# Modulated 1-D convolutions on one core: the whole of G ahead of the eviction of S, VectorE's side work at the iteration's end

## Chip, cores and metric

The kernel runs on one core of a Trainium2 chip. The metric is the device time of one execution in microseconds (us). All times below are us unless marked ns. The engines are TensorE (PE; its weight loads are listed as PEld), VectorE (DVE), ScalarE (ACT), GpSimd (POOL) and SyncE (SP, which issues the DMAs).

## What is computed

For 128 samples of 64 channels by 1024 positions, four convolution layers (64 to 64 channels, three taps, the weights scaled per sample by a style vector and then normalised per output channel) are chained, and the input is added to the result. The types are same, upsample (stride 2 transposed, then blurred), same, downsample (blurred, then stride 2). No nonlinearity stands between them.

```python
s = style @ mw.T + mb
weight = SCALE * w * s[:, None, :, None]
demod = lax.rsqrt(jnp.sum(weight * weight, axis=(2, 3)) + EPS)
weight = weight * demod[:, :, None, None]
...
for i, typ in enumerate(TYPES):
    out = _layer(out, style, weights[i], biases[i], mod_w[i], mod_b[i], typ)
...
x = x + _L0_cond_ref(x, cond_512, ...)
```

## The kernel before

**The idea.** Since nothing nonlinear stands between the layers, the kernel multiplies the four layers' weights together for each sample, into one filter of nine taps, and applies that to the input. Only the few positions at both row ends, where the padding of the single layers shows, are computed apart, layer by layer, for all samples at once ("row ends").

**The work of one sample group.** Samples are taken four at a time: q counts 32 groups (NQ). A group has two rows r or s of results, each in its own PSUM bank. The steps, with the names in the code:

- `scale3`, `stage1_a`, `stage1_b` (lines 415, 461, 473): the weights of the last two layers are multiplied on TensorE into psS (line 428). ScalarE evicts four blocks of S (line 399), VectorE evicts two more in two instructions, one per bank (line 481: "the eviction of S"), GpSimd then adds two blocks of S (line 484). The bank pair of psS is the pool `ps_w`, which has one buffer: psS, psR and psW of the different groups take turns in it.
- `share_sums`, `share`, `share_copy` (lines 499, 515, 524): in some iterations part of stage 2 is computed once for several blocks: VectorE adds blocks of S (line 501), TensorE multiplies them into spare columns of psA (line 506), and ScalarE copies the result into a new psR (line 529), which lies in the banks that psS has just left.
- `stage2_rest` or `stage2_taps` (lines 535, 577): TensorE multiplies S with the blurred second layer E onto psR (line 506, or 589 without sharing); ScalarE evicts R (line 399).
- `r_sums` (GpSimd, line 638), `stage3_b`, `stage3_a` (TensorE, line 621): the first layer's weights come in; ScalarE evicts the filter Wf.
- `combine_a`, `combine_b` (VectorE): sums of filter taps, H.
- `in_g01`, `in_g2`, `in3`, `in04`, `in1`, `in2`: the input X of a group lies as three planes of every third position. VectorE makes the planes of G from X, one in `in_g2` (684 elements in each partition) and two in `in_g01` (1376), both line 712; then T3 = X − X (`in3`, line 761), T04 (`in04`, line 790), and on GpSimd T12 (`in1`, line 776, and `in2`, line 781), which need G. G has one buffer, X two.
- `conv0` to `conv4` (line 803): TensorE multiplies the five T with Wf or H into psA and Y, in the manner of a fast convolution with five products for three outputs. `sum1` (line 851) and `sum2` (lines 860 and 862) combine these on VectorE; `outputs` (line 880) scales them on ScalarE and starts the stores.

**The order.** Nothing is scheduled automatically: each engine does its instructions in the order in which the code issues them, and semaphores make it wait for others. `turn_of(q)` (line 1483) is one iteration: it works for group q (last products), n = q + 1 (first products), c = q + 2 (stages 2 and 3, input) and s = q + 4 (stage 1). It runs for q = 4 to 28; q = 4 is the entry (`entry`), and 0 to 3 and the last three groups have code of their own. Sharing is on for 4 < q < 28 (line 1370).

**Side work.** The row ends and the per-sample constants of later groups are spread over the iterations. `SIDE` (line 1334) is a table from q to a few VectorE instructions: for q = 4 the last step of an inverse root (`var_newton`), for 5 to 7 `small_rest` (for 7 also `table_b` on GpSimd), for 8 to 27 pieces of the row ends (13 `setup1`, none for 14 and 19). In iterations 4, 5 and 6 there is also a memset of some columns of Y (line 1524), onto which the small matmuls (`small`, line 1290) add later in the iteration. In 10, 14, 15 and 19 TensorE does row-end matmuls (`SLOTS`, line 1271) behind the sharing matmuls.

**Where it stands.** On VectorE one iteration is: `sum2`, `combine_a` and `combine_b`, `in04`, `share_sums`, `in_g2`, then `side(SIDE, q)` and the memset, then the eviction of S, then `in_g01`, `sum1`, `in3`, and the next iteration's `sum2`. On TensorE it is stage 2 of c, conv2 of q, stage 3, conv4, conv3 of n, stage 1, conv0, the rest of stage 1, the sharing matmuls, conv1 of n, the small matmuls, and again stage 2.

Of the kernel before, what the change touches and what calls it, by code (L numbers as in the profile page):

```python
# [63 lines left out]
def kernel(  # L64
# [18 lines left out]
    nc_v, nc_a, nc_g = nc.vector, nc.scalar, nc.gpsimd  # L83
# [57 lines left out]
    def load(q, planes=slice(0, 3), cs=range(2)):  # L141

        if q < NQ:
            at = slice(planes.start * PL, planes.stop * PL)
            for c in cs:
                nc.sync.dma_start(Xs[q % NX][:, c, at], x[2 * q + c, :, at])
# [165 lines left out]
    def var_newton(bs, ls=slice(0, NL)):  # L312

        newton(var[:, ls, bs], dm[:, ls, bs], nw[:, ls, bs])
# [44 lines left out]
    def table_b(bs):  # L359
        table(nc_g, tb, bs, slice(0, 2), slice(2, 4), oc[:, bs], 1.0)  # L360
# [199 lines left out]
    def stage2(q, pool=None, engs=(nc_a, nc_a), between=None):  # L560
        if q in shared_ps:
            ps = stage2_rest(q)
        else:
            ps = opened.pop(q, None)
            taps = range(9) if ps is None else range(3, 9)
            ps = stage2_taps(q, taps, ps or unit(pool or ps_w, f"psR{q}"))
        if between:
            between()
        t = r_pool.tile([P, 2, 9, C], F32, tag="R", name=f"R{q}")
        for r in range(2):  # L570
            scaled_copy(engs[r], flat(t[:, r, :7]), ps[r][:, : 7 * C], tC[:, q, r : r + 1])
        chain[q] = t
        return ps
# [62 lines left out]
    def r_sums(q, eng):  # L636
        t = chain[q]
        eng.tensor_add(t[:, :, 7:9], t[:, :, 2:6:3], t[:, :, 3:7:3])
# [3 lines left out]
    def stage3_b(q, ps):  # L642

        new_w(q)
        t = chain[q]
        plan = (
            (slice(0, 3), w0s[2][:, 2, :], slice(0, 7, 3)),
            (slice(0, 2), w0s[2][:, 1, :], slice(1, 5, 3)),
            (slice(0, 2), w0s[2][:, 0, :], slice(2, 6, 3)),
            (slice(3, 4), w0s[0][:, 0, :], slice(0, 1)),  # L650
            (slice(4, 5), w0s[1][:, 0, :], slice(1, 2)),
            (slice(4, 5), w0s[1][:, 1, :], slice(0, 1)),
            (slice(5, 7), w0s[0][:, 1, :], slice(7, 9)),
        )
        for i, (at, weight, slots) in enumerate(plan):
            same_row(blocks(ps, at), weight, t, slots, i == 0, i == len(plan) - 1)
        pw = shared_w[q] = unit(ps_w, f"psW{q}")
        src = blocks(ps, slice(5, 7))
        for i, f in enumerate((1.0, 1.0 / 3.0)):
            for dst, v in zip(blocks(pw, slice(i, i + 3, 2)), src):  # L660
                scaled_copy(nc_a, dst, v, f)
        stage3_out(q, ps, 0, 5)
# [48 lines left out]
    def sum_of(out, x, f, y, op=ALU.add):  # L711
        nc_v.scalar_tensor_tensor(out, x, f, y, op0=ALU.mult, op1=op)  # L712
# [6 lines left out]
    def combine_a(q):  # L719

        chain.pop(q)
        a, b, c, h1, h2, h3 = taps(q)
        sum_of(h1, c, -2.0, a)
        residual(q)
        sum_of(h3, h1, 1.0 / 6.0, b)

    def combine_b(q, steps=range(3)):

        a, b, c, h1, h2, h3 = taps(q)
        plan = (h2, c, -0.5, a), (h1, b, -3.0, h2, ALU.subtract), (h2, h2, -1.0 / 3.0, b)  # L730
        for i in steps:
            sum_of(*plan[i])
# [10 lines left out]
    def plane(buf, i, pairs=BOTH_PAIRS):  # L743

        at = PL * (2 - i) if i < 3 else PL * 2 + 1
        return buf[:, pairs, at : at + NJ]

    def t_tile(q, tag):
        if (q, tag) not in Ts:
            Ts[q, tag] = tpool.tile([P, 2, 1 + (tag != "T3"), PL], F32, tag=tag, name=f"{tag}_{q}")  # L750
        return Ts[q, tag]

    def g_tile(q):
        if q not in Gs:
            Gs[q] = gpool.tile([P, 2, 3 * PL], F32, tag="G", name=f"G{q}")
        return Xs[q % NX], Gs[q]
# [6 lines left out]
    def in_g01(q, pairs=BOTH_PAIRS):  # L763
        if q < NQ:
            X, g = g_tile(q)
            sum_of(g[:, pairs, PL:], X[:, pairs, : 2 * PL], 0.5, X[:, pairs, PL:], ALU.subtract)
# [6 lines left out]
    def in1(q, eng):  # L773
        if q < NQ:
            t, g = t_tile(q, "T12"), Gs[q]
            eng.tensor_add(t[:, :, 0, :NJ], plane(g, 2), plane(g, 1))  # L776

    def in2(q, eng):
        if q < NQ:
            t, g = t_tile(q, "T12"), Gs[q]  # L780
            eng.tensor_sub(t[:, :, 1, :NJ], plane(g, 2), plane(g, 1))  # L781
# [46 lines left out]
    def open_a(q):  # L828
        A[q] = ps_conv.tile([P, 2, 512], F32, tag="u", name=f"psA{q}")
        return banks(q)  # L830
# [22 lines left out]
    def conv2(q, *groups):  # L853
        product(q, 2, banks(q), groups or range(K))

    def sum2(q, steps=(0, 1)):
        if 0 in steps:
            m3 = m3c.pop(q)
            for s, a in enumerate(banks(q)):
                sum_of(Y[:, s, :NB], m3[:, s], 3.0, a[:, :NB])  # L860
        for s, a in parts(q) if 1 in steps else ():
            nc_v.tensor_sub(y1w[q][:, s], y1w[q][:, s], a)

    def conv4(q, *groups):
        product(q, 4, Y_banks, groups or range(K))

    def conv0(q, *groups):
        product(q, 0, banks(q), groups)
# [149 lines left out]
    def setup_x(h):  # L1018
        bs = slice(h * HB, (h + 1) * HB)
        nc_v.tensor_tensor(Xm[:, bs], Xe[:, bs], spread(sc[:, 0, bs], 8), op=ALU.mult)  # L1020
# [43 lines left out]
    def add0(s):  # L1064
        dst = Ye[s][:, :, 1:7]
        nc_v.tensor_tensor(dst, dst, spread(c0, 6), op=ALU.add)
# [211 lines left out]
    def high(n):  # L1278
        return Y[:, 1, NB + 4 : NB + 4 + n]

    SMALL = {
        1: (0, PART[1]),
        2: (1, PART[1]),
        3: (2, PART[1]),
        4: (0, REST),
        5: (1, REST),
        6: (2, REST),
    }
# [10 lines left out]
    def small_rest(q):  # L1299
        l, bs = SMALL[q]  # L1300
        const_rest(l, bs, high(bs.stop - bs.start))

    def layers(i, j):
        return REST, slice(i, j)
# [19 lines left out]
    def last_factors():  # L1324
# [9 lines left out]
    SIDE = {  # L1334
        4: lambda: var_newton(*layers(3, 4)),
        5: lambda: small_rest(4),
        6: lambda: small_rest(5),
        7: lambda: (small_rest(6), table_b(REST)),
        8: lambda: setup_x(0),
        9: lambda: setup_x(1),  # L1340
        10: setup0,
        11: lambda: add0(0),
# [21 lines left out]
    def side(work, q):  # L1364
        work.get(q, lambda: None)()
# [117 lines left out]
    def turn_of(q):  # L1483
        n, c, s = q + 1, q + 2, q + 4
        entry = q == FIRST
        stage2(c)
        if entry:
            sum2(q)
            conv4(q)
            combine_a(n)  # L1490
            r_sums(c, nc_v)
        else:
            conv2(q)
            r_sums(c, nc_g)
            sum2(q)
            in2(n, nc_g)
        side(TABLES, q)
        for i in range(3):
            load(c + 1, slice(i, i + 1))
        stage3_b(c, open_a(n))  # L1500
        if entry:
            conv0(q, 0, 1)
        else:
            combine_a(n)
            conv4(q)
        stage3_a(c)
        combine_b(n)
        conv3(n)
        if entry:
            copy_m3(n)  # L1510
            stage1_a(s)
        outputs(q, 2)
        if not entry:
            if s < NQ:
                stage1_a(s)
            copy_m3(n)
        in04(n)
        if sharing(q):
            share_sums(c + 1)
        in_g2(c)  # L1520
        side(SIDE, q)
        if q in SMALL:
            l, bs = SMALL[q]
            nc_v.memset(high(bs.stop - bs.start), 0.0)
        conv0(q, *((2,) if entry else range(K)))
        if entry:
            conv1(n, 0, 1)
        outputs(q, 1)
        if s < NQ:
            stage1_b(s)  # L1530
        in_g01(c)
        if sharing(q):
            share(c + 1, banks(q))
            share_copy(c + 1)
        outputs(q, 0)
        if q in SLOTS:
            matmuls, width, rest = SLOTS[q]
            slot(matmuls, width, Y_banks)
            rest()
        if s == NQ:  # L1540
            slot(ends3, 3, unit(ps_w, "psE"), 3)
            rest3()
        conv1(n, *((2,) if entry else range(K)))
        if q in SMALL:
            small(q)
        sum1(n)
        in3(c)
        side(LATE, q)
        if s == NQ:
            in04(c)  # L1550
        in1(c, nc_g)
        if s + 1 < NQ:
            scale3(s + 1)

# [5 lines left out]
    q, n, c = NQ - 3, NQ - 2, NQ - 1  # L1560
# [32 lines left out]
    q, n = NQ - 2, NQ - 1  # L1593
# [128 lines left out]
```

## Time and profile before

| | before |
|---|---|
| device time, median of 3 runs | 475.72 us (475.56 to 475.97) |
| span of the profiled execution | 475.5 us |
| PE busy | 469.7 us, 99% of the span |
| weight loads (PEld) | 349.5 us, 74% |
| VectorE busy | 417.3 us, 88% |
| ScalarE busy | 312.0 us, 66% |
| GpSimd busy | 165.8 us, 35% |

The span runs from the first to the last instruction of one profiled execution; the device time of that execution is not listed apart from the three runs, whose lowest is 475.56. A row of a time line reads: start, length, engine, line, operation, what it writes `<-` what it reads, shapes, number of instructions merged into the row, and in brackets the idle time of the engine just before, with the engine, tile and line that ended it. Rows of weight loads show when TensorE takes up a step better than those of matmuls, whose ends are modelled. An ordinary iteration in the middle of the span lasts 13.84 us.

### The profile page before, as it was taken

Reading aid. Unit: us, or ns where it says so; the run is one execution under the profiler, and the core shown is the slowest. Engines: PE = TensorE matmul, PEld = TensorE weight load, DVE = VectorE, ACT = ScalarE, POOL = GpSimd, SP = SyncE. Lnnn points to the kernel's source line nnn. Section 1 sums busy time; section 2 is a strip of 40 time slices with the busy share of each in tenths; the row PEclk is TensorE's granted clock in tenths of the full one; section 3 lists DMA queues with packets and bytes.
Section 4 is the critical chain, followed back from the end, with each engine's and each line's share of the span. In section 5 each row is a group of like instructions: output and inputs, shape, how many; then the busy total and the mean of one; then the engine's idle time right before and its main releaser. Section 6 shows DMA issues by size and latency. Waiting matters only on the chain.

```text
span 475.5 us, 26771 instructions
## 1 busy us (share of the span) xinstructions
PE 469.7 (99%) x11932; PEld 349.5 (74%) x11932; DVE 417.3 (88%) x694; ACT 312.0 (66%) x711; POOL 165.8 (35%) x200
## 2 busy tenths in 40 slices
PE   9999999999999999999999999999999999999996
PEld 6987788777678876677776677766788787876653
DVE  3889998879989998899979899979998999999896
ACT  4565657577766676766667666667666777766464
POOL 3634033664444342233432233422333423243200
PEclk9999999999999999999999999999999999999999
DMA  5237456535445554345544454543555544455225
GB/s 176 71 115 224 150 151 180 152 113 177 139 145 166 166 166 136 123 150 169 163 150 126 130 168 152 178 124 121 152 164 169 164 145 147 148 152 161 80 91 193
DMA packets 52707, 70.71 MB, mean 149 GB/s; under 512 B 6000, under 2 KB 50672, under 8 KB 52592
## 3 DMA queue, kind: packets, MB, share of 16 engines
q1 hardware_dynamic: 52368, 68.78, 46.3%
q8 instruction: 93, 1.52, 1.4%
q10 hardware_dynamic: 224, 0.22, 0.1%
q14 instruction: 22, 0.18, 0.1%
HBM read 35.36 MB, written 33.62 MB: 145 GB/s over the span
## 4 chain that ended last, share of the span: by engine, by line
PE 99%; DVE 0%; ACT 0%; issue 0%
PE psA L803 47%; PE Y L803 12%; PE psR L506 9%; PE psW L621 7%; PE psA L621 7%; PE psS L428 6%; PE psR L589 5%; PE psA L506 2%; PE Y L1044 2%; PE Y L183 1%; PE Y L379 1%; PE psM L220 0%; PE psE L1044 0%; PE Y L255 0%; DVE o L882 0%; PE psM L255 0%
## 5 line engine op out<-in xcount | busy, mean ns | idle before, releaser
L803 PE MATMUL psA<-T,H 64*64 64x340 f32 x2304 | 185.9, 446 | 0.0
L803 PEld LDWEIGHTS psA<-T,H 64*64 64x64 f32 x2304 | 90.7, 133 | 46.9 <-issue 2.5
L712 DVE SCALAR_TENSOR_TENSOR G<-X 128x1376 f32<-128x1376 f32 (+2 forms) x65 | 78.0, 1206 | 0.2
L776 POOL TENSOR_TENSOR T<-G 128x684 f32<-128x684 f32 x28 | 46.3, 1652 | 73.7 <-DVE G L712 73.7
L484 POOL TENSOR_TENSOR S<-S 128x128 f32<-128x128 f32 x28 | 21.6, 772 | 139.7 <-ACT S L399 139.6
L399 ACT ACTIVATE R<-psR,tC 128x448 f32<-128x448 f32 x63 | 36.6, 631 | 43.6 <-PE psR L506 25.8
L803 PE MATMUL psA<-T,Wf 64*64 64x340 f32 x768 | 63.7, 446 | 0.0
L803 PE MATMUL Y<-T,Wf 64*64 64x340 f32 x768 | 62.4, 451 | 0.0
L712 DVE SCALAR_TENSOR_TENSOR Y<-m,psA 128x340 f32<-128x340 f32 x62 | 32.0, 516 | 28.2 <-PE psA L803 26.9
L399 ACT ACTIVATE psW<-psA 128x128 f32<-128x128 f32 x100 | 19.3, 268 | 49.1 <-PE psA L621 45.0
L790 DVE TENSOR_TENSOR T<-G 128x1368 f32<-128x1368 f32 (+1 forms) x33 | 50.8, 1541 | 0.0
L399 ACT ACTIVATE Wf<-psW,t 128x256 f32<-128x256 f32 (+2 forms) x76 | 32.7, 480 | 26.7 <-PE psW L621 26.4
L761 DVE TENSOR_TENSOR T<-X 128x684 f32<-128x684 f32 x32 | 47.7, 1492 | 0.0
L506 PE MATMUL psR<-S,E 64*64 64x64 f32 (+1 forms) x1472 | 46.8, 237 | 0.0
L781 POOL TENSOR_TENSOR T<-G 128x684 f32<-128x684 f32 x28 | 46.5, 1660 | 0.0
L428 PEld LDWEIGHTS psS<-wd,w2n 64*64 64x64 f32 x1120 | 35.1, 133 | 12.9 <-issue 0.3
L506 PEld LDWEIGHTS psR<-S,E 64*64 64x64 f32 x1472 | 39.5, 134 | 4.9 <-ACT psR L529 0.2
L803 PEld LDWEIGHTS Y<-T,Wf 64*64 64x64 f32 x768 | 30.3, 132 | 16.8
L803 PEld LDWEIGHTS psA<-T,Wf 64*64 64x64 f32 x768 | 29.8, 133 | 14.5
L880 ACT ACTIVATE o<-psA,tb,td 128x340 f32<-128x340 f32 x63 | 37.1, 648 | 5.0 <-PE psA L803 2.8
L880 ACT ACTIVATE o<-y,tb,td 128x340 f32<-128x340 f32 x62 | 38.5, 678 | 0.0
L880 ACT ACTIVATE o<-Y,tb,td 128x340 f32<-128x340 f32 x62 | 36.1, 639 | 2.8 <-PE Y L803 2.0
(180 smaller groups left out, 840.4 us busy)
## 6 DMA issues: line engine op xcount, KB each, us to landing
out<-o SPq DMA_DIRECT2D x191, 170.0 KB, 2.6
X<-in_x SPq DMA_DIRECT2D x150, 172.0 KB, 3.4
X<-in_x SPq DMA_DIRECT2D x14, 516.0 KB, 5.0
par<-in_params SPq DMA_DIRECT2D x3, 192.0 KB, 3.8
Xe<-in_x_ends SPq DMA_DIRECT2D x1, 512.0 KB, 4.5
out<-Oe SPq DMA_DIRECT2D x2, 96.0 KB, 2.1
out<-o ACTq DMA_DIRECT2D x1, 170.0 KB, 2.8
par<-in_params SPq DMA_DIRECT2D x1, 160.0 KB, 2.7
```

What stands on the lines that cost most here:

```text
L399: nc_a.activation(dst, src, AF.Copy, scale=f)
L428: nc.tensor.matmul(ps[r][cols, at * C : (at + n) * C], weight[rows], wd[c if r == 0 else 1 - c][rows, taps], start=first, stop=last, skip_ ...
L506: nc.tensor.matmul(dst[r][cols], weight[rows], st[c if r == 0 else 1 - c][rows, slots, :], start=False, stop=last, skip_group_check=True,)
L589: nc.tensor.matmul(ps[r][cols, lo * C : (lo + m) * C], E[rows, e + 2, :], src[rows, a, :], start=(n == 0), stop=(n == 8), skip_group_check ...
L621: nc.tensor.matmul(dst[r][cols], weight[rows], t[rows, c, slots, :], start=first, stop=last, skip_group_check=True,)
L712: nc_v.scalar_tensor_tensor(out, x, f, y, op0=ALU.mult, op1=op)
L761: nc_v.tensor_sub(t[:, pairs, 0, :NJ], plane(X, 3, pairs), plane(X, 1, pairs))
L776: eng.tensor_add(t[:, :, 0, :NJ], plane(g, 2), plane(g, 1))
L781: eng.tensor_sub(t[:, :, 1, :NJ], plane(g, 2), plane(g, 1))
L790: nc_v.tensor_sub(t[:, pairs, :, :NJ], both(a, PL), both(b, 1))
L803: nc.tensor.matmul(ps[s][cols, :NB], w, Ts[q, tag][rows, c, i, g : g + NB], start=(g == 0 and (m == 3 or alone)), stop=(g == K - 1), skip_ ...
L880: nc_a.activation(dst, src, AF.Identity, bias=add, scale=d3)
```

## The change

`in_g01(c)` moves from behind `stage1_b` to just behind `in_g2(c)`, so VectorE makes all of G in one piece and evicts S after it. The side work of iteration q moves to the end of iteration q − 1, behind T3 and, in the program, behind GpSimd's `in1`; only the entry does its own in the old place (now behind `in_g01`), and its successor's at its end. The memset of Y moves behind the eviction of S. No instruction is added or removed, and the orders of TensorE, ScalarE and SyncE are the same; on GpSimd only the two instructions of `table_b` move, from behind `in2` and three small factors of iteration 7 to behind `in1` of iteration 6.

```diff
@@ turn_of(q) @@
         in_g2(c)
-        side(SIDE, q)
-        if q in SMALL:
-            l, bs = SMALL[q]
-            nc_v.memset(high(bs.stop - bs.start), 0.0)
+        in_g01(c)
+        if entry:
+            side(SIDE, q)
         conv0(q, *((2,) if entry else range(K)))
         if entry:
             conv1(n, 0, 1)
         outputs(q, 1)
         if s < NQ:
             stage1_b(s)
-        in_g01(c)
+        if q in SMALL:
+            l, bs = SMALL[q]
+            nc_v.memset(high(bs.stop - bs.start), 0.0)
         if sharing(q):
...
         if s == NQ:
             in04(c)
         in1(c, nc_g)
+        side(SIDE, q + 1)
         if s + 1 < NQ:
             scale3(s + 1)
```

VectorE in the middle of iteration 18, before. L501 is `share_sums`, the two G are `in_g2` (342 in two halves) and `in_g01` (688 in two halves), L1102 is the side work, L481 the eviction of S, y is `sum1`, T is T3, Y is `sum2`:

```order
L501 TENSOR_TENSOR S_5374<-S_5374 128x2x128
L712 SCALAR_TENSOR_TENSOR G_5652<-X_105 128x2x342
L1102 SCALAR_TENSOR_TENSOR Ue_162<-b1s,Ue_162 64x64 x2
L1102 SCALAR_TENSOR_TENSOR Ue_163<-b1s,Ue_163 64x64 x2
L481 SCALAR_TENSOR_TENSOR S_5644<-psS_0_5630,tB,S_5644 128x128
L481 SCALAR_TENSOR_TENSOR S_5644<-psS_1_5631,tB,S_5644 128x128
L712 SCALAR_TENSOR_TENSOR G_5652<-X_105 128x2x688
L712 SCALAR_TENSOR_TENSOR y_19_5718<-psA_5537,m_19_5647 128x680
L761 TENSOR_TENSOR T_20_5720<-X_105 128x2x342
```

The same place of the changed kernel (the numbers in the names differ a little):

```order
L501 TENSOR_TENSOR S_5375<-S_5375 128x2x128
L712 SCALAR_TENSOR_TENSOR G_5656<-X_105 128x2x342
L712 SCALAR_TENSOR_TENSOR G_5656<-X_105 128x2x688
L481 SCALAR_TENSOR_TENSOR S_5648<-psS_0_5634,tB,S_5648 128x128
L481 SCALAR_TENSOR_TENSOR S_5648<-psS_1_5635,tB,S_5648 128x128
L712 SCALAR_TENSOR_TENSOR y_19_5718<-psA_5541,m_19_5651 128x680
L761 TENSOR_TENSOR T_20_5720<-X_105 128x2x342
```

The two instructions of the eviction now stand behind 1376 elements of G in each partition where four short ones stood; those four are done at the end of iteration 17, behind that iteration's T3. VectorE in iteration 4 (the entry), as a difference of the two orders; L279 to L281 are `var_newton`, L1524 and L1532 the memset of Y:

```order
 L712 SCALAR_TENSOR_TENSOR G_1828<-X_105 128x2x342
+L712 SCALAR_TENSOR_TENSOR G_1828<-X_105 128x2x688
 L279 TENSOR_TENSOR nw<-dm,var 128x96
 L280 SCALAR_TENSOR_TENSOR nw<-nw,dm 128x96
 L281 SCALAR_TENSOR_TENSOR dm<-nw,dm 128x96
-L1524 MEMSET Y 128x96
 L481 SCALAR_TENSOR_TENSOR S_1818<-psS_0_1804,tB,S_1818 128x128
 L481 SCALAR_TENSOR_TENSOR S_1818<-psS_1_1805,tB,S_1818 128x128
-L712 SCALAR_TENSOR_TENSOR G_1828<-X_105 128x2x688
+L1532 MEMSET Y 128x96
```

The memset has gone from ahead of the eviction to behind it, and G's second instruction the other way.

## Prediction

> **What bounds the kernel now.** I read the page's chain first, then busy time by stretches of one iteration, then the time lines of VectorE, ScalarE and TensorE's weight loads inside it. The chain that ended last is TensorE almost alone:
>
> ```profile
> PE 99%; DVE 0%; ACT 0%; issue 0%
> ```
>
> The next view cuts two neighbouring iterations at VectorE's first subtraction into Y (`sum2`), the one spot where it waits for TensorE each time. Columns: stretch, its length, then busy time of PE, PEld, DVE, ACT, POOL.
>
> ```profile
> 277.73:291.57 13.84, 13.84 (x392) 9.79 (x388) 13.01 (x19) 9.86 (x23) 4.80 (x5) 1.00 0.51 161
> 291.57:305.52 13.95, 13.95 (x392) 10.13 (x388) 13.35 (x22) 9.86 (x23) 4.87 (x5) 1.00 0.49 150
> ```
>
> The first is iteration 17, the second iteration 18. PE is busy throughout both, yet the second is 0.11 longer with the same 392 matmuls. So "busy" hides a stall, and the stall is what this change works on. VectorE in iteration 17, from the G plane of `in_g2` on:
>
> ```profile
> 284.44 0.86 DVE L712 SCALAR_TENSOR_TENSOR G<-X 128x684 f32<-128x684 f32 x1
> 285.22 1.01 DVE L1093 SCALAR_TENSOR_TENSOR Ue<-b1s,Ue 128x576 f32<-128x576 f32 x1
> 286.25 0.61 DVE L481 SCALAR_TENSOR_TENSOR S<-psS,tB,S 128x128 f32<-128x128 f32 x2
> 286.78 1.58 DVE L712 SCALAR_TENSOR_TENSOR G<-X 128x1376 f32<-128x1376 f32 x1
> 288.28 0.86 DVE L712 SCALAR_TENSOR_TENSOR y<-psA,m 128x680 f32<-128x680 f32 x1
> 289.05 1.85 DVE L761 TENSOR_TENSOR T<-X 128x684 f32<-128x684 f32 x1
> 291.57 0.52 DVE L712 SCALAR_TENSOR_TENSOR Y<-m,psA 128x340 f32<-128x340 f32 x1 [0.67 <-PE psA L803]
> ```
>
> VectorE runs without a gap until 290.90 and then waits 0.67 for TensorE. What hangs on the eviction of S: ScalarE's `share_copy` (L529) writes psR into the PSUM banks that psS held, and TensorE's stage 2 (L506) adds onto what it wrote. The same iteration:
>
> ```profile
> 286.69 0.63 ACT L529 COPY psR<-psA 128x256 f32<-128x256 f32 x2 [0.24 <-DVE S L481]
> ...
> 287.39 0.44 PEld L506 LDWEIGHTS psR<-S,E 64*64 64x64 f32 x8
> ...
> 288.53 1.65 POOL L776 TENSOR_TENSOR T<-G 128x684 f32<-128x684 f32 x1 [2.92 <-DVE G L712]
> ```
>
> TensorE takes up stage 2 at 287.39, just after the copy. Iteration 18, with longer side work, shows what follows when S is later:
>
> ```profile
> 300.48 0.61 DVE L481 SCALAR_TENSOR_TENSOR S<-psS,tB,S 128x128 f32<-128x128 f32 x2
> ...
> 300.92 0.63 ACT L529 COPY psR<-psA 128x256 f32<-128x256 f32 x2 [0.62 <-DVE S L481]
> ...
> 301.33 0.41 PEld L506 LDWEIGHTS psR<-S,E 64*64 64x64 f32 x6 [0.23 <-ACT psR L529]
> ...
> 305.52 0.52 DVE L712 SCALAR_TENSOR_TENSOR Y<-m,psA 128x340 f32<-128x340 f32 x1 [0.39 <-PE psA L803]
> ```
>
> Here S starts 8.91 after the Y subtraction (300.48 − 291.57), the first stage 2 weight load comes 0.85 later (301.33) and waits for the copy, and the next Y subtraction comes 5.04 after S (305.52 − 300.48). In iteration 17 S came at 8.52 (286.25 − 277.73) and cost nothing: there the load stands at 9.66 (287.39 − 277.73), TensorE's own pace. **So S has until about 9.66 − 0.85 = 8.81; each later microsecond is a microsecond on the iteration.**
>
> **The change, part by part.** *G ahead of S.* `in_g2` ends at 285.30. Before, 0.95 of side work stood between it and S; now 1.58 of `in_g01` does. S then starts at 286.88 at the earliest, 9.15 after the Y subtraction. But GpSimd's addition in S (L484) falls into just this place. Iteration 10, where the side work holds the same instruction twice, shows what it does to the VectorE instruction behind `in_g2`:
>
> ```profile
> 182.25 0.86 DVE L712 SCALAR_TENSOR_TENSOR G<-X 128x684 f32<-128x684 f32 x1
> ...
> 182.59 0.83 POOL L484 TENSOR_TENSOR S<-S 128x128 f32<-128x128 f32 x1 [5.15 <-ACT S L399]
> ...
> 183.03 0.47 DVE L1025 TENSOR_TENSOR a<-dm 64x64 f32<-64x64 f32 x1
> 183.43 0.18 DVE L1026 COPY c<-c0f 64x64 f32<-64x64 f32 x1
> 183.62 0.22 DVE L1025 TENSOR_TENSOR a<-dm 64x64 f32<-64x64 f32 x1
> ...
> 187.13 0.44 PEld L506 LDWEIGHTS psR<-S,E 64*64 64x64 f32 x8
> ```
>
> The first copy of L1025, beside GpSimd's addition, took 0.47, the second, after it, 0.22: a hold of 0.25. Will `in_g01` be held too? Ends: 0 and 0.25, taken 0.25, since it too reads two tensors of SBUF and takes the very place of the held row.
> The Trainium skill ("SBUF — State Buffer", section "Who interferes with whom") says that a VectorE instruction with two SBUF inputs and a GpSimd instruction that reads SBUF exclude each other, the one that starts first holding the port to its end. By that rule the hold is there; an estimate without the rule would be the 9.15 above. This trace agrees with it in the 0.47 against 0.22.
> So S starts at 9.15 + 0.25 = 9.40, and with iteration 18's 5.04 behind it an iteration lasts 14.44 instead of 13.84: **+0.60** (+0.35 without the hold). The delay doesn't pile up: the next iteration's VectorE work starts from its own Y subtraction, which waits for TensorE.
>
> How many iterations? `share_copy` runs in 23 of them, two copies each:
>
> ```profile
> L529 ACT COPY psR<-psA x46: 347/360/387, 114.5 to 428.4; 128x256 f32<-128x256 f32 x46
> ```
>
> Four of these (10, 14, 15, 19) have the row-end matmuls between the sharing matmuls and stage 2. In iteration 10 `in_g2` ends at 183.11; S would start at 183.11 + 1.83 = 184.94 and the load could follow at 185.8, well before 187.13: nothing lost. Of the 19 left, iteration 18 already pays 0.11, so it adds 0.49; 5 and 6 have a memset and small matmuls (below); 16 are plain: 16 × 0.60 = 9.6.
>
> *The memset of Y behind S* (iterations 4, 5, 6). The small matmuls (L1295) wait for it, and TensorE reaches stage 2 only behind them. Iteration 4, with no sharing:
>
> ```profile
> 100.74 0.14 DVE L1524 MEMSET Y<- 128x96 f32 x1 [2.39 <-ACT o L880]
> 100.79 0.53 DVE L481 SCALAR_TENSOR_TENSOR S<-psS,tB,S 128x128 f32<-128x128 f32 x2
> ...
> 100.99 0.22 PEld L1295 LDWEIGHTS Y<-c0f,wsum 64*64 64x64 f32 x4 [0.46 <-issue]
> 101.13 0.17 PEld L589 LDWEIGHTS psR<-S,E 64*64 64x64 f32 x2
> ```
>
> The memset's start moves from 100.74 to behind S, at the latest 101.32: between nothing, if S no longer waits and starts earlier, and 0.58. Stage 2 waits for all of S anyway, so I take 0.35. In 5 and 6 S ends at about 10.0 after the Y subtraction, the memset at 10.1, the small load can come at 10.2 (0.11 behind it, as in iteration 4), and stage 2 a further 0.14 to 0.30 behind (101.13 − 100.99 here, 129.81 − 129.51 in iteration 6):
>
> ```profile
> 129.51 0.42 PEld L1295 LDWEIGHTS Y<-cc,wsum 64*64 64x64 f32 x4
> 129.81 0.29 PEld L506 LDWEIGHTS psR<-S,E 64*64 64x64 f32 x8
> ```
>
> With the Y subtraction of iteration 6 at 119.86 its stage 2 load stood at 9.95; it would stand at 10.35 to 10.5: 0.5 each, 1.0 for both.
>
> *Side work behind T3*: costed at nothing. VectorE now ends S at 10.0, waits for the conv1 result, and does `sum1` (0.86). T3 took 1.85 because GpSimd's T12 sum (288.53 to 290.18) ran beside it; that sum now starts about 1.2 earlier, right behind G, so T3 should need about 0.87, like the G plane of equally many elements. VectorE is then through with T3 near 12.1 and with 1.4 of side work at 13.5, before the Y subtraction at 14.44. Were that cover gone, the side work's whole length would delay sum2, 0.7 to 1.4 an iteration. GpSimd's part of it, `table_b` of iteration 7, is moved ahead of `r_sums`:
>
> ```profile
> L332 POOL TENSOR_SCALAR tb<-oc 64x48 f32<-64x48 f32 x2 | 0.7, 342 | 5.4 <-DVE oc L977 5.3
> ```
>
> Two short ones of 0.34, behind a T12 sum that ends earlier. The loads of X only find their planes read sooner.
>
> Sum: 9.6 + 0.5 + 1.0 + 0.35 = 11.45. The profiled span of 475.5 lies 0.2 under the median of 475.72. So 475.7 + 11.4 = **487.1**.
>
> **Rivals.**
> 1. *No hold on `in_g01`*: +0.35 an iteration: 16 × 0.35 + 0.24 (iteration 18) + 0.6 + 0.35 = 6.8, **482.5**. For it: no G instruction stands behind L484 in this trace. Against: the 0.25 above.
> 2. *The S eviction itself is held* by the T12 sum, which now starts 0.17 behind G (288.53 against 288.36). S's second half would wait out 1.65 of it, about 1.5 more in each of 19 iterations, about 28 on top: **515**. Against: `sum1` at 288.28, also PSUM with SBUF, took 0.86 beside the same sum, no longer than its elements need.
> 3. *TensorE doesn't stall*, or the edit leaves S's start where it was because S waits for something later anyway: **475.8**. Against: iteration 18 lost 0.11 at a delay of only 0.39 more.
> 4. *Faster*: T3 loses its wait for GpSimd, 1.85 − 0.87 = 0.98 in each iteration. If VectorE paced the iteration, that would outweigh the 0.60, and the 16 plain ones would gain 0.38 each: **469.6**. It decides as soon as the Y subtraction no longer waits for TensorE. In the rows it waits 0.67 and 0.39, so VectorE's time is spare there.
> The same rule of the Trainium skill (section "Who interferes with whom") stands behind rival 4: it frees T3 once GpSimd is done earlier, and the trace agrees that T3 is long only beside the sum.
>
> **How the numbers follow.** The forecast has a chance of 0.75, rival 1 0.11, rival 2 0.03, rival 3 0.05, rival 4 0.06. About 0.2% (0.95) is what a measurement can tell from no change. Faster is rival 4, 0.06; same is rival 3, 0.05; slower is the rest, 0.89. The forecast itself reaches from 484.5 (memsets free, some iterations late on TensorE's own account) to 490 (0.7 an iteration); with rival 1 the range is 481 to 490, which leaves out rivals 2, 3 and 4 and the edges.
>
> **What would show it.** Plain iterations of 14.4 instead of 13.84; S about 9.4 after the Y subtraction, G's big instruction at 1.83 instead of 1.58; each L529 waiting for S, and PEld L506 with a wait for L529 in about 19 iterations; T3 near 0.87; the wait of the Y subtraction for PE longer than 0.9. Iterations 10, 14, 15 and 19 unchanged. I am wrong if stage 2's load stays at 9.66, or if the Y subtraction stops waiting for TensorE.

## The result, and the profile after

The changed kernel takes **483.97 us** (median of 4 runs, 483.51 to 485.05), the kernel before 475.85 us beside it (4 runs, 475.56 to 477.07): a ratio of 1.0162, 95% interval 1.014 to 1.0183, or 8.1 us slower. The profiled execution took 484.11 us with a span of 482.3 us.

The same two iterations as in the prediction, 17 and 18, cut at the Y subtraction (stretch, length, then busy time of PE, PEld, DVE, ACT, POOL; the last three columns are the granted TensorE clock, the DMA engines' busy share and GB/s):

```profile
281.07:295.35 14.28, 14.28 (x392) 10.63 (x388) 12.35 (x23) 9.86 (x23) 4.79 (x5) 1.00 0.51 152
295.35:309.75 14.40, 14.32 (x392) 10.62 (x388) 11.52 (x19) 9.86 (x23) 4.92 (x5) 1.00 0.49 158
```

They were 13.84 and 13.95. PE still reads as busy all through, with the same 392 matmuls and the granted clock at 1.00: the loss doesn't show in PE's share (99% before and after), only in the lengths. VectorE in iteration 17:

```profile
287.43 0.42 DVE L501 TENSOR_TENSOR S<-S 128x256 f32<-128x256 f32 x1
287.76 2.63 DVE L712 SCALAR_TENSOR_TENSOR G<-X 128x684 f32<-128x684 f32 x2
290.32 0.59 DVE L481 SCALAR_TENSOR_TENSOR S<-psS,tB,S 128x128 f32<-128x128 f32 x2
291.34 0.87 DVE L712 SCALAR_TENSOR_TENSOR y<-psA,m 128x680 f32<-128x680 f32 x1 [0.43 <-PE psA L803]
292.12 0.86 DVE L761 TENSOR_TENSOR T<-X 128x684 f32<-128x684 f32 x1
292.90 1.12 DVE L1102 SCALAR_TENSOR_TENSOR Ue<-b1s,Ue 64x64 f32<-64x64 f32 x4
295.35 1.07 DVE L712 SCALAR_TENSOR_TENSOR Y<-m,psA 128x340 f32<-128x340 f32 x2 [1.32 <-PE psA L803]
```

The eviction of S starts 9.25 after the Y subtraction (290.32 − 281.07), where it was 8.52. The copy and the weight load behind it, and GpSimd:

```profile
290.74 0.63 ACT L529 COPY psR<-psA 128x256 f32<-128x256 f32 x2 [0.94 <-DVE S L481]
```
```profile
291.15 0.41 PEld L506 LDWEIGHTS psR<-S,E 64*64 64x64 f32 x6 [0.55 <-ACT psR L529]
```
```profile
288.13 0.81 POOL L484 TENSOR_TENSOR S<-S 128x128 f32<-128x128 f32 x1 [5.21 <-ACT S L399]
290.56 1.64 POOL L776 TENSOR_TENSOR T<-G 128x684 f32<-128x684 f32 x1 [1.62 <-DVE G L712]
```

The load comes 0.83 behind S, at 10.08 instead of 9.66, and now waits for the copy; the next Y subtraction comes 5.03 behind S (295.35 − 290.32). The table of waits says the same over the whole span (total, times, longest):

```profile
DVE Y L712 <- PE psA L803: 45.2, 28, 2.5
...
ACT psR L529 <- DVE S L481: 21.9, 23, 1.1
...
PEld psR L506 <- ACT psR L529: 9.1, 17, 0.7
```

Seventeen waits of stage 2 for the copy: the 16 plain iterations and iteration 18. VectorE's own wait for PE has grown by 18.3 to 45.2 us (26.9 before): it has more time to spare than before, not less. The page's chain speaks of less:

```profile
PE 36%; DVE 1%; issue 0%; ACT 0%; DVEq 0%; ACTq 0%
```

These shares add up to 37%, because the chain could be followed back only as far as about 305 us. Such a row describes the end of the span, not the whole; the stretches above are what can be relied on.

By iterations, the changed profile against 13.84 where before was undisturbed: 16 plain ones at 14.26 to 14.30, 16 × 0.43 = 6.9; iteration 18 0.45; iterations 5 and 6 0.34 and 0.27 (against their own 14.01); iteration 4 0.40 (17.40 against 17.00). Sum 8.4, against the 8.1 measured. Iterations 10, 14, 15 and 19 last what they did, to 0.01.

### The profile page after: what moved, and what is told of

Same layout as the page of the kernel before. It is cut to its first block, busy times and chain, and to the rows that moved or that the text cites. A ratio compares the mean times of both kernels' runs of the same rounds, so it can differ in the third digit from the quotient of the medians.

```text
span 482.3 us, 26771 instructions
## 1 busy us (share of the span) xinstructions
PE 475.3 (99%) x11932; PEld 355.3 (74%) x11932; DVE 400.9 (83%) x694; ACT 312.8 (65%) x711; POOL 165.9 (34%) x200
## 5 line engine op out<-in xcount | busy, mean ns | idle before, releaser
L803 PE MATMUL psA<-T,H 64*64 64x340 f32 x2304 | 188.0, 447 | 0.0
L803 PEld LDWEIGHTS psA<-T,H 64*64 64x64 f32 x2304 | 98.9, 133 | 40.5 <-issue 2.5
L712 DVE SCALAR_TENSOR_TENSOR G<-X 128x1376 f32<-128x1376 f32 (+2 forms) x65 | 82.6, 1308 | 0.2
L712 DVE SCALAR_TENSOR_TENSOR Y<-m,psA 128x340 f32<-128x340 f32 x62 | 32.0, 516 | 46.4 <-PE psA L803 45.2
L506 PEld LDWEIGHTS psR<-S,E 64*64 64x64 f32 x1472 | 46.7, 134 | 11.5 <-ACT psR L529 9.1
L506 PE MATMUL psR<-S,E 64*64 64x64 f32 (+1 forms) x1472 | 53.7, 241 | 0.1
L781 POOL TENSOR_TENSOR T<-G 128x684 f32<-128x684 f32 x28 | 46.4, 1658 | 0.0
L638 POOL TENSOR_TENSOR R<-R 128x256 f32<-128x256 f32 x24 | 17.4, 726 | 68.5 <-ACT R L399 68.5
L803 PEld LDWEIGHTS psA<-T,Wf 64*64 64x64 f32 x768 | 28.8, 133 | 15.0
L621 PEld LDWEIGHTS psA<-R,w0s 64*64 64x64 f32 x1000 | 37.6, 134 | 1.5
```

The costliest lines, as they stand in the source:

```text
L506: nc.tensor.matmul(dst[r][cols], weight[rows], st[c if r == 0 else 1 - c][rows, slots, :], start=False, stop=last, skip_group_check=True,)
L621: nc.tensor.matmul(dst[r][cols], weight[rows], t[rows, c, slots, :], start=first, stop=last, skip_group_check=True,)
L803: nc.tensor.matmul(ps[s][cols, :NB], w, Ts[q, tag][rows, c, i, g : g + NB], start=(g == 0 and (m == 3 or alone)), stop=(g == K - 1), skip_ ...
```

## The experiments

Diffs are against the changed kernel. "S at" and "period" are the start of the eviction of S after the Y subtraction and the time to the next one. Lines shift by a few where a kernel adds a helper.

### 1. Only the side work moves

```diff
         in_g2(c)
-        in_g01(c)
         if entry:
             side(SIDE, q)
...
             nc_v.memset(high(bs.stop - bs.start), 0.0)
+        in_g01(c)
         if sharing(q):
```

> Side work stays at the iteration's end and the memset of Y behind S, but G's two planes go back behind the eviction of S. Theory (all of the loss is S coming at 9.24 instead of 8.81 or earlier after the Y subtraction): S starts near 8.2, plain iterations last 13.84, the time is 475.5 to 476.5, near the kernel before. Rival (the loss comes from the side work at the end, or from the memset, delaying the Y subtraction): plain iterations stay near 14.27 and the time near 484.

Measured: 478.83 (478.19 to 478.94) against 475.80, ratio 1.0066 (1.005 to 1.0081). Neither number. The plain iterations are back at 13.84 with S at 8.17, so what they lost came from G's place. But three iterations are longer, 17 above all (VectorE, then GpSimd, then weight loads):

```profile
277.36:293.29 15.93, 15.10 (x440) 10.81 (x432) 15.01 (x23) 10.57 (x28) 6.76 (x6) 1.00 0.53 160
```
```profile
288.54 1.86 DVE L761 TENSOR_TENSOR T<-X 128x684 f32<-128x684 f32 x1
290.32 2.94 DVE L1102 SCALAR_TENSOR_TENSOR Ue<-b1s,Ue 64x64 f32<-64x64 f32 x4
293.29 1.07 DVE L712 SCALAR_TENSOR_TENSOR Y<-m,psA 128x340 f32<-128x340 f32 x2
```
```profile
288.01 1.66 POOL L776 TENSOR_TENSOR T<-G 128x684 f32<-128x684 f32 x1 [2.77 <-DVE G L712]
290.77 0.73 POOL L638 TENSOR_TENSOR R<-R 128x256 f32<-128x256 f32 x1 [1.10 <-ACT R L399]
291.45 1.68 POOL L781 TENSOR_TENSOR T<-G 128x684 f32<-128x684 f32 x1
```
```profile
294.41 1.35 PEld L803 LDWEIGHTS Y<-T,Wf 64*64 64x64 f32 x24 [2.19 <-DVE Y L712]
```

G is late, so the T12 sum is late and T3 is held (1.86). The four short instructions of the side work then start at 290.32, just ahead of GpSimd's `r_sums` (L638) and `in2` (L781), and take 2.94 beside them, where the changed kernel's took 1.12. The Y subtraction comes without any wait for PE in front of it, and TensorE waits 2.19 for it. Iteration 17 costs 2.09, iteration 7, where an instruction into H is held beside `in2` (1.30 instead of 0.55), 0.56, iteration 4, whose memset stays behind S here, 0.40, and iteration 18, which lost its side work, gives back 0.11: 2.94 of the 3.03 measured. Elsewhere the side work costs nothing at the end, T3 held or not: the Y subtraction still waits at least 0.28 for PE. In the changed kernel, where G ahead of S frees T3, the same two pieces cost nothing beyond the delay of S.

### 2. GpSimd's addition in S moved out of G's way

```diff
+    def add_s(t):
+        nc_g.tensor_add(t[:, :, 2], t[:, :, 2], t[:, :, 0])
...
-        nc_g.tensor_add(t[:, :, 2], t[:, :, 2], t[:, :, 0])
+        if not FIRST < q - 4 < NQ:
+            add_s(t)
...
         in1(c, nc_g)
+        if not entry and s < NQ:
+            add_s(whole[s])
         side(SIDE, q + 1)
```

> The changed kernel, with GpSimd's addition in S issued behind its T12 sum, so that it no longer runs beside VectorE's G. Theory (G's large instruction is held 0.26 by that addition, and each microsecond of S is one of the iteration): the G instruction takes 1.58 instead of 1.85, S starts near 8.98, plain iterations last 14.02, the time is 479.3 (479 to 480). Rival (the hold costs nothing, because S waits for something else): 484.

Measured: 478.91 (478.69 to 479.75) against 475.80, ratio 1.0074 (1.0058 to 1.009), as the theory of the hold had it. A plain iteration:

```profile
350.83:364.84 14.01, 14.01 (x392) 10.71 (x388) 11.85 (x20) 9.87 (x23) 4.40 (x5) 1.00 0.54 165
```
```profile
357.52 2.36 DVE L716 SCALAR_TENSOR_TENSOR G<-X 128x684 f32<-128x684 f32 x2
359.80 0.60 DVE L484 SCALAR_TENSOR_TENSOR S<-psS,tB,S 128x128 f32<-128x128 f32 x2
```

G's pair takes 2.36 instead of 2.63, S starts at 8.97 (359.80 − 350.83) and the period is 14.01: 0.27 less in each, one for one. In the 19 iterations that lose time the hold is worth 19 × 0.27 = 5.1 us; the medians differ by 483.97 − 478.91 = 5.06. The 0.17 that a plain iteration still loses is G's own length ahead of S.

### 3 and 4. G cut by columns: half ahead of S, or all but 172 elements

```diff
+    def in_g_cols(q, i, j):
+        if q < NQ:
+            X, g = g_tile(q)
+            sum_of(g[:, :, PL + i : PL + j], X[:, :, i:j], 0.5, X[:, :, PL + i : PL + j], ALU.subtract)
...
-        in_g01(c)
+        in_g_cols(c, 0, 344)
...
             nc_v.memset(high(bs.stop - bs.start), 0.0)
+        in_g_cols(c, 344, 2 * PL)
```

The other one has 602 for 344.

> The changed kernel, with G's two planes made in two instructions: 688 elements in each partition ahead of S, 688 behind it. Same work, one more instruction. T12 needs only the first. Theory: S starts near 8.5, under the limit of 8.81, plain iterations last 13.84, T3 stays short (0.87), the time is 475.5 to 476. Rival (the loss is due to the side work at the end): 484. Rival (VectorE's freed time is worth something once S is early): under 474.

> As the split at 688, with 1204 elements ahead of S and 172 behind it. Theory (slope one beyond 8.81): S starts near 9.05, plain iterations last 14.08, the time is 480.5 (480 to 481). A step instead of a slope would give 476 or 484.

Measured: half ahead, 480.12 (478.96 to 481.68), ratio 1.0096 (1.0077 to 1.0115), a miss; all but 172 ahead, 480.87 (480.52 to 481.21), ratio 1.0111 (1.009 to 1.0131), near its number. In the first, S did come at 8.52, within its 8.81, and yet (VectorE, GpSimd, weight loads):

```profile
264.00:278.08 14.08, 14.05 (x392) 10.02 (x388) 13.24 (x20) 9.87 (x23) 5.05 (x5) 1.00 0.44 139
```
```profile
272.54 0.60 DVE L481 SCALAR_TENSOR_TENSOR S<-psS,tB,S 128x128 f32<-128x128 f32 x2
273.06 2.10 DVE L712 SCALAR_TENSOR_TENSOR G<-X 128x688 f32<-128x688 f32 x1
275.08 0.85 DVE L712 SCALAR_TENSOR_TENSOR y<-psA,m 128x680 f32<-128x680 f32 x1
```
```profile
272.78 1.65 POOL L781 TENSOR_TENSOR T<-G 128x684 f32<-128x684 f32 x1 [0.90 <-DVE G L712]
```
```profile
276.05 1.08 PEld L808 LDWEIGHTS psA<-T,H 64*64 64x64 f32 x18
```

The first half, columns 0 to 344 in each, is plane 1, all that the T12 sum still needs, so GpSimd starts at 272.78, ahead of the second half of G, which then takes 2.10. `sum1` behind it starts at 11.08 (275.08 − 264.00) and ends near 11.9, and conv2's weight load (L808) comes at 12.05 (276.05 − 264.00). That is a second deadline, on `sum1`, which the theory did not have; the next Y subtraction comes 3.00 behind the start of `sum1`. Iterations 7, 17 and 18 lose more (14.51, 14.30 and 14.19); what their further loss is was not tried apart. In the other kernel S at 9.06 alone gives 9.06 + 5.03 = 14.09, its period, but its `sum1` was as late (11.08), so that run doesn't separate the two deadlines.

### 5. Only G moves

```diff
         in_g01(c)
-        if entry:
-            side(SIDE, q)
+        side(SIDE, q)
...
         in1(c, nc_g)
-        side(SIDE, q + 1)
```

> G whole ahead of S as in the change, but the side work stays in its iteration, now behind G and ahead of S (the memset of Y behind S, as in the change). Theory (each microsecond that S is later than 8.81 after the Y subtraction costs one): S comes at 9.24 plus the side work, 0.25 less than its rows before since G takes the hold, so 0.3 to 1.1 later than in the change in the plain iterations, about 0.55 on average, 16 to 17 times: about 9 more than the change, 493 (491 to 495). Rival (the side work at the end is a good part of the change's loss, so that it is better in the old place): at most 484.

Measured: 504.46 (502.67 to 508.18) against 475.88, ratio 1.0618 (1.058 to 1.0655), worse by 11 than expected. Iteration 18:

```profile
309.05:325.93 16.88, 14.32 (x392) 10.62 (x388) 13.79 (x22) 9.84 (x23) 4.77 (x5) 1.00 0.41 131
```
```profile
318.29 2.56 DVE L1102 SCALAR_TENSOR_TENSOR Ue<-b1s,Ue 64x64 f32<-64x64 f32 x4
320.89 0.61 DVE L481 SCALAR_TENSOR_TENSOR S<-psS,tB,S 128x128 f32<-128x128 f32 x2
```
```profile
318.54 1.63 POOL L776 TENSOR_TENSOR T<-G 128x684 f32<-128x684 f32 x1 [1.62 <-DVE G L712]
```

The T12 sum starts behind G and falls on the side work, which takes 2.56 instead of 1.12 and stands ahead of S. S comes at 11.84 and the period is 16.88, again S + 5.04; elsewhere 9.84 gave 14.87 and 9.91 gave 14.94. Against the changed kernel 15 of the 16 plain iterations (all but 13) cost 8.5 together, near the 9 expected. The miss lies in iterations 5, 6, 10, 13, 15 and 18, where S comes at 11.13 to 11.84 and which cost 11.3 more together. One of them stands off the line: in iteration 5 S at 11.21 gave 17.78, 1.5 beyond S + 5.03. TensorE's weight loads had waited 2.49 there, and the granted clock (third figure from the end) was 0.54 in the stretch behind the wait:

```profile
118.78:122.50 3.72, 3.72 (x114) 3.72 (x118) 1.48 (x2) 2.22 (x5) 0.00 (x0) 0.54 0.47 122
```

Iterations 6 and 18, after waits of 2.41 and 3.16, show 1.00, so what lowers the clock these runs don't show. So the second half of the change saves about 20 us of the first half's 29 (504.46 against 483.97): the two halves can't be added up from either alone.

### 6. G cut the other way: plane 0 ahead of S, plane 1 behind

```diff
-        in_g01(c)
+        in_g_cols(c, PL, 2 * PL)
         if entry:
             side(SIDE, q)
+        if q in SMALL:
+            l, bs = SMALL[q]
+            nc_v.memset(high(bs.stop - bs.start), 0.0)
...
-        if q in SMALL:
-            l, bs = SMALL[q]
-            nc_v.memset(high(bs.stop - bs.start), 0.0)
+        in_g_cols(c, 0, PL)
```

> Like the split at 688, but the other plane of G goes first, so that GpSimd's T12 sum cannot start before the second plane is done, and the memset of Y stands in its old place ahead of S. Theory (the split at 688 lost its 0.23 an iteration because the T12 sum held G's second part 1.3, which made sum1 late, for which conv2 waits): the second part now takes 0.87, sum1 starts at 10.27, conv2's load stays at 11.82 and plain iterations last 13.84. Time 475.5 to 477, nothing lost to the kernel before but what the side work at the end may cost. Rival (it is the extra instruction or the side work at the end): plain iterations at 14.07, 480.

Measured: 475.76 (12 runs, 474.63 to 477.30) against 475.88, ratio 1.0008 (0.9993 to 1.0023).

```profile
276.55:290.39 13.84, 13.84 (x392) 9.79 (x388) 12.97 (x23) 9.84 (x23) 4.81 (x5) 1.00 0.55 168
```
```profile
285.08 0.60 DVE L481 SCALAR_TENSOR_TENSOR S<-psS,tB,S 128x128 f32<-128x128 f32 x2
285.60 0.86 DVE L712 SCALAR_TENSOR_TENSOR G<-X 128x688 f32<-128x688 f32 x1
286.81 0.87 DVE L712 SCALAR_TENSOR_TENSOR y<-psA,m 128x680 f32<-128x680 f32 x1 [0.35 <-PE psA L808]
```

S at 8.53 as in experiment 3, and as many elements behind it, but the T12 sum now has to wait for the second part. That part takes 0.86 instead of 2.10, `sum1` starts at 10.26 and the period is 13.84. With the 2.10 of experiment 3 this shows the second deadline. It also shows that nothing is to be won: with both deadlines kept and the side work at the end, the kernel is as fast as before and no faster, since TensorE alone sets 13.84.

### 7. Side work at the end, but for iterations 7 and 18

```diff
         in_g2(c)
-        in_g01(c)
-        if entry:
+        if entry or q in (7, 18):
             side(SIDE, q)
...
+        in_g01(c)
         if sharing(q):
...
-        side(SIDE, q + 1)
+        if q + 1 not in (7, 18):
+            side(SIDE, q + 1)
```

> The first experiment (side work at the end, G behind S), with the side work of iterations 7 and 18 left in its old place. Theory (those two alone collide with GpSimd's work at the iteration's end: 2.1 at the end of iteration 17, 0.55 around that of 6): 476.2 (475.8 to 476.6). Rival (the 3.0 is spread over all iterations): 478.5.

Measured: 475.91 (12 runs, 474.96 to 477.83) against 475.88, ratio 1.0008 (0.9994 to 1.0021). Iterations 7 and 17 are back at 13.84 and 13.85, iteration 18 at 13.95; iteration 4 keeps its 0.40 (17.39). So 2.5 of experiment 1's three microseconds (2.09 + 0.56 − 0.11) came from these two pieces of side work; the 0.40 of iteration 4 is in this kernel too, and at 0.03 between the medians it is lost in the spread of the runs.

### 8. The memset back ahead of S

```diff
+        if q in SMALL:
+            l, bs = SMALL[q]
+            nc_v.memset(high(bs.stop - bs.start), 0.0)
         conv0(q, *((2,) if entry else range(K)))
...
-        if q in SMALL:
-            l, bs = SMALL[q]
-            nc_v.memset(high(bs.stop - bs.start), 0.0)
```

> The changed kernel with the memset of Y back ahead of S in iterations 4, 5 and 6 (behind G). Theory: iteration 4 lasts 17.0 again instead of 17.4, since the small matmuls wait for the memset; 5 and 6 stay within 0.1 of 14.3, since S is 0.1 later and the memset no longer follows it. Rival (the 0.4 of iteration 4 comes from G ahead of S): 17.4.

Measured once: 483.68, span 481.9. Iteration 4 is back at 16.99, so its 0.40 is the memset's. Iterations 5 and 6 last 14.48 and 14.34, no shorter than the changed kernel's 14.35 and 14.27; iteration 5, with S at 9.51, misses the 0.1 expected. There the memset's place hardly counts, S does.

## Why the prediction was right, and where it was off

The side, the mechanism and the iterations it falls on were right: 484.0 lies within 481 to 490, 3.1 below the 487.1. But it lies below 484.5 too, where the forecast proper was to end, and nearer to rival 1's 482.5 than to 487.1. The range held it because it had been widened for rival 1, which experiment 2 rules out: that is luck. The number alone would not have told the two apart.

*S's deadline.* "S has until about 9.66 − 0.85 = 8.81; each later microsecond is a microsecond on the iteration." The runs set S at these places:

| S at | period | kernel |
|---|---|---|
| 8.17 | 13.84 | experiment 1 |
| 8.53 | 13.84 | experiment 6 |
| 8.66 | 13.84 | experiment 6, iteration 18 |
| 8.91 | 13.95 | before, iteration 18 |
| 8.97 | 14.01 | experiment 2 |
| 9.06 | 14.09 | experiment 4 |
| 9.25 | 14.28 | changed kernel |
| 9.37 | 14.40 | changed kernel, iteration 18 |
| 9.84 | 14.87 | experiment 5 |
| 11.84 | 16.88 | experiment 5, iteration 18 |

Flat up to 8.66, then S + 5.03 or 5.04 throughout; that line meets 13.84 at 8.81. Experiment 3 (S at 8.52 to 8.54, period 14.06 to 14.08) is not in the table, because there `sum1` sets the period, and iteration 5 of experiment 5 is not, because of its clock. In iteration 18 of before, from which the prediction took its 5.04, `sum1` was late as well:

```profile
302.50 0.86 DVE L712 SCALAR_TENSOR_TENSOR y<-psA,m 128x680 f32<-128x680 f32 x1
```

It starts 10.93 after the Y subtraction, and with experiment 3's 3.00 that alone makes 13.93 of the 13.95. So this row could not tell the two limits apart, and that its 5.04 belongs to S was in part luck. It is borne out by the changed kernel and experiment 2, whose `sum1` starts at 10.27 in most iterations.

*The hold on `in_g01`.* Taken at 0.25, measured at 0.27 (experiment 2). Rival 1, no hold, is out; what it would look like is experiment 2's kernel. Here the Trainium skill ("SBUF — State Buffer", section "Who interferes with whom") had said that the two engines exclude each other on such instructions, and these runs agree.

*The mis-sized term: "So S starts at 9.15 + 0.25 = 9.40".* It started at 9.25. The 9.15 counts `in_g2` and `in_g01` end to end, 285.30 + 1.58. But the prediction's own rows show that VectorE's rows overlap: `in_g2` runs from 284.44 for 0.86, to 285.30, and the next row starts at 285.22; `in_g01` ends at 288.36 and the next row starts at 288.28. Each of these begins 0.08 before the end of the one ahead of it. Counted by starts, S is at 285.22 + 1.58 − 0.08 = 286.72, 8.99 after the Y subtraction (experiment 2 shows 8.97), and with the hold 9.26. So a plain iteration costs 0.43 and not 0.60: 16 × 0.17 = 2.7 of the 3.1 that the forecast was too high.
The Trainium skill ("Perfetto Trace Analysis", section "Optimizing Scalar/DVE Operations") says that part of an instruction's profiled latency, the acknowledgement of its writes, overlaps with the next instruction. The trace agrees as to the overlap, with 0.08 a row; what the overlapped part is it doesn't show.

*Memsets.* Iteration 4 was taken at 0.35 and cost 0.40, and experiments 6 and 8, whose memset stands ahead of S, take it back (16.99 each). Iterations 5 and 6 were taken at 0.5 each and cost 0.34 and 0.27, 0.4 less together. The prediction had them wait for the memset alone; experiment 8, with the memset ahead of S, loses no less there, so S's own delay is enough for it.

*Iterations 10, 14, 15 and 19 lose nothing; 18 loses less than the plain ones.* Right, to 0.01 and with 0.45 for 0.49.

*"Side work behind T3: costed at nothing."* Right for this kernel, with the cover named: T3 takes 0.86 and the Y subtraction still waits 1.32 behind the longest side work. Where T3 stays long, as in experiment 1, the price given, 0.7 to 1.4 an iteration, was wrong both ways: most pieces cost nothing, since the Y subtraction still waited for PE, and the one of iteration 18, done at the end of 17, cost 2.09, because it is itself held by GpSimd.

*Rival 2, the eviction held by the T12 sum.* Out: two instructions in 0.59 with the sum starting beside the second (290.56). *Rival 3, no stall.* Out: 17 waits of stage 2 for the copy. *Rival 4, VectorE paces.* T3 was freed as it said, but the wait of the Y subtraction for PE grew from 0.67 and 0.39 to 1.32 and more; and experiment 6, which frees VectorE without a late S, gains nothing.

*"The profiled span of 475.5 lies 0.2 under the median."* The difference is right, but the two are not the same execution. Device time is about 1.8 us above the span of the same run (484.11 and 482.3 here), and the 11 runs of before beside experiment 1 have spans of 472.5 to 475.1, so the profiled execution was one of its longer ones: iterations 8, 22 and 26 of it last 13.99, 14.23 and 13.98 with S in time. The sum did not suffer, since each term was counted against the 13.84 of an undisturbed iteration.

## What to carry to other kernels

Find for each eviction the time from which it costs, as the matmul stage behind it minus what lies between; up to there an engine's order is free, beyond it each tenth counts in every iteration. There can be more than one such limit: here S had one and `sum1` another. Sum a chain on one engine from start to start and not by adding row lengths. Before moving VectorE work with two SBUF inputs, look at what GpSimd does at the new place, and at what of GpSimd the move sets off earlier.

## What the runs showed of the hardware

In these runs a VectorE instruction with two SBUF inputs that starts behind a GpSimd one waits out all of it, whatever its own length: in experiment 3 the GpSimd sum ends at 274.43 (272.78 + 1.65) and G's half at 275.16, 0.73 later, and experiment 1's T3 ends 0.73 behind its sum (290.40 and 289.67). In experiment 4 a piece of 172 elements, beside the same sum, took 1.56:

```profile
275.12 1.56 DVE L712 SCALAR_TENSOR_TENSOR G<-X 128x172 f32<-128x172 f32 x1
```
```profile
274.85 1.64 POOL L781 TENSOR_TENSOR T<-G 128x684 f32<-128x684 f32 x1 [1.44 <-DVE G L712]
```

So a small piece is not a cheap one there. GpSimd waits in its turn: its addition in S took 0.81 beside G, and 0.46 in experiment 2, where it ran beside `sum1`, which reads PSUM:

```profile
289.05 0.46 POOL L474 TENSOR_TENSOR S<-S 128x128 f32<-128x128 f32 x1
```

Expected from the rows of before was a hold of the instruction behind `in_g2`; that four short instructions could be stretched from 1.12 to 2.94 was not.
